# Early loads issued behind the last transposed keys, and one more stage between an expert's gather and its transposes

## The chip, the cores and the metric

The kernel runs on one core of one Trainium2 chip. The metric is the device time of the whole program in microseconds (us), as the median of the runs shown. A core has five engines that each work through their own instruction list in order and wait for one another by semaphores: TensorE (PE in the profile), VectorE (DVE), ScalarE (ACT), GpSimd (POOL) and SyncE (SP), which in this kernel only issues DMAs. POOL issues DMAs as well, beside its arithmetic.

## The reference

A layer norm of x (4 sequences of 2048 tokens, 256 wide) feeds two branches whose outputs are added to x: a gated linear attention with 8 heads, and a mixture of 64 experts, of which each token uses 8.

```python
xn = _layernorm(x)
# attention: q, k (8 heads x 128), v (8 heads x 64), alpha = sigmoid((xn @ Wg + bg) / 16)
state = alpha * state + k[..., None] * v[:, None, :]      # step by step over each sequence
out_t = einsum('bhk,bhkv->bhv', q, state)
attn  = (out * sigmoid(xn @ Wog)) @ Wo
# experts, over all n = 8192 tokens
scores = sigmoid(xn @ gate_w.T)
topk_idx = 8 of 64 experts, out of the best 4 of 8 groups (scores + bias decide)
topk_w   = scores of those 8, normalised, times 2.5
pos      = rank of the token among those of its expert, in the order of the tokens
buf[e, pos] = xn[token]  for pos < CAP                    # CAP = 256 rows an expert
y   = einsum(silu(buf @ w_gate) * (buf @ w_up), w_down)
moe[token] += y[e, pos] * topk_w
return x + attn + moe
```

## The kernel before

**Blocks.** The tokens are cut into 32 blocks of 256 (two chunks of 128). `block(s)` does the attention of block s and, between its parts, the projections of block s+1: `gate` (output gate), `values`, `queries` and `keys`, each for a half of the heads. `unit_a` makes the decays and scores of one half and chunk, `unit_m` multiplies them, `unit_d` makes the outputs and the new state. After each part comes a `step()`, twelve in a full block and seven in the last one.

**Side work.** `step()` first runs what lies in `side`: for the first half of the program that is the routing (`front`, `decays`, `back` for 16 batches of 512 tokens). `front` normalises a batch, transposes it with a DMA (`xT`, line 363), stores it, and multiplies it with the router's weights (`lg` on PE). The batches also leave the counts in `cnt_d`, and the rows to be gathered (tokens and weights, 1280 bytes each) in `xw_d`.

**Experts.** When the side work is done (at block 17 of 0 to 31), 64 experts go through a pipeline that `step()` drives: every 12/5 steps a new expert starts, and every expert already under way moves on by one stage. This interval is called a period below. `fetch` issues three loads of the expert's weights (`w`, on SP) and two gathers of its 256 rows (`xe`, indirect DMAs on POOL). The stages that follow are `expert_in` (eight PE transposes of the rows into `xet`, and the split of weights and rows into high and low parts), `expert_mid` (the two products, `gu`, and the activation), `expert_out` (the third product, `yp`, and the scaled rows `y` on ACT), and `expert_add` (two scatter-adds of `y` into the output, on POOL). `behind_adds` makes every scatter-add, and every write of an attention block (`finish`, `out_dram<-res`, on POOL as well), wait until the last two scatter-adds before it have landed. Ahead of the gathers, `look(e)` finds the row numbers of expert e; for each eighth expert (`NF = 8`) `steps` first loads two tables of counts `c` and subtracts them into `dd`. Once all experts have started, they move on by a stage with every step.

**Buffers.** `w` has three buffers, `xe` four, `y` four, `el` three, `xs` two, `c` one of each kind.

**The loads of a block.** `block(s)` opens with `load_block(s+1)` (`xs`, the transposed tokens; `aj` and `mv`, the decay vectors) and `load_el(s+1, 0)`; `load_el(s+1, 1)` comes after the second half of the keys. `el` is 512 KB, read by `queries` (`qt` on DVE) and by the copies `wall`, which are on POOL for blocks below 16 and on DVE above. `keys` ends with a DMA that transposes the keys of a half (`kt`, line 837), which `unit_d` multiplies.

**Order.** Tile's scheduler fixes each engine's order when the program is built, from the dependences and from when it takes each instruction to be ready; a load whose buffer is free can thus stand on SP well ahead of its place in the text. `tc.issue_after(ins)` adds the rule that what the block traces on the engine of `ins` is issued after `ins`, without a wait for it to finish.

Of the kernel before, what the change touches and what calls it, by code (L numbers as in the profile page):

```python
# [8 lines left out]
F32 = mybir.dt.float32  # L9
# [10 lines left out]
P = 128  # L20
NT = 8192
NTL = NT // 128
# [3 lines left out]
E, CAP, I = 64, 256, 128  # L26
# [10 lines left out]
XW = D + E  # L37
# [15 lines left out]
DGROUPS = ((0, 1), (1, 1), (2, 2), (4, 4), (8, 4), (12, 4))  # L53

STEPS = 12
NF = 8
AHEAD = 2
EXPERTS = 5

# [10 lines left out]
def gla_moe_kernel(ctx: ExitStack, tc: tile.TileContext, x, Wq, Wk, Wv, Wo, Wg, bg, Wog,  # L70
                   gate_wT, gate_bias, w_gate, w_up, w_down, out):
    nc = tc.nc
# [10 lines left out]
    cnt_d = dram.tile([(NTL + 1) * E, P], F16, name="cnt_d")  # L83
# [31 lines left out]

    dd_t = [const.tile([NTL, NF, P + 2], F16, name=f"dd{i}") for i in range(2)]

# [22 lines left out]
    made = {}  # L140
# [404 lines left out]

    moe = {}

    def steps(g):

        both = []  # L550
        for t in range(2):
            c = moe["m1"].tile([NTL, NF, P], F16, name=f"c{t}")
            nc.sync.dma_start(out=c, in_=cnt_d[t * E:(t + NTL) * E, :].rearrange(
                "(t e) i -> t e i", e=E)[:, g * NF:(g + 1) * NF, :])
            both.append(c)
        nc.vector.tensor_tensor(dd_t[g % 2][:, :, 0:P], both[1], both[0], ALU.subtract)

    def find(e):

        m2 = moe["m2"]
        before = m2.tile([NTL, CAP], F16, name="before")
        nc.vector.tensor_scalar(before, srow, cex[:, e:e + 1], None, ALU.is_ge)
        row = ps["mo"].tile([P, 2, P + 1], F32, tag="mo", name="row")
        for f in range(2):
            nc.tensor.matmul(row[:, f, :], lhsT=before[:, f * P:(f + 1) * P],
                             rhs=dd_t[e // NF % 2][:, e % NF, 0:P + 1], start=True, stop=True)
        le_ = m2.tile([P, 2, P], F16, name="le_")
        place = m2.tile([P, 2], F32, name="place")  # L570
        for f in range(2):
            nc.vector.tensor_scalar(le_[:, f], row[:, f, 0:P], slot[:, f:f + 1], None, ALU.is_le, ALU.add,
                                    accum_out=place[:, f:f + 1])
        nc.vector.tensor_tensor(idx[:, e], row[:, :, P], place, ALU.add)

    def look(e):
        if e < E:
            if e % NF == 0:
                steps(e // NF)
            find(e)  # L580

    def fetch(e):
        w4 = moe["w4"]
        w = w4.tile([P, 6, I], F32, name="w", bufs=3)
        nc.sync.dma_start(out=w[:, 0:2], in_=w_gate[e].rearrange("(c p) i -> p c i", p=P))
        nc.sync.dma_start(out=w[:, 2:4], in_=w_up[e].rearrange("(c p) i -> p c i", p=P))
        nc.sync.dma_start(out=w[:, 4:6].rearrange("p c i -> p (c i)"), in_=w_down[e])
        xe = w4.tile([P, 2, XW], F32, name="xe", bufs=4)
        for f in range(2):
            nc.gpsimd.indirect_dma_start(  # L590
                out=xe[:, f, :], out_offset=None, in_=xw_d[:, :],
                in_offset=bass.IndirectOffsetOnAxis(ap=idx[:, e, f:f + 1], axis=0))
        return dict(w=w, xe=xe)

    def expert_in(e, m):

# [33 lines left out]
    def expert_split(e, m):  # L630
        hh = moe["m2"].tile([P, CAP], F32R, name="hh")
        hl = moe["m2"].tile([P, CAP], F32R, name="hl")
        nc.scalar.copy(hh, m["hs"])
        moe["late"].append((nc.vector, hl, m["hs"], hh))
        m["h"] = (hh, hl)
# [31 lines left out]
        tc.declare_no_dep(two[1], two[0], reason="the halves of an expert share no row")  # L667
        adds.extend(two)

    expert_stages = [expert_in, expert_mid, expert_out, expert_add]  # L670

    def expert_late():

# [4 lines left out]
    def expert_step(new):  # L678

        q = moe["at"]  # L680
        mids = []
        for it in list(q):
            e, m, st = it
            if st == len(expert_stages):
                continue
            expert_stages[st](e, m)
            if st == 1:
                mids.append((e, m))
            it[2] += 1
        for e, m in mids:  # L690
            expert_split(e, m)
        moe["at"] = [it for it in q if it[2] < len(expert_stages)]
        if new and moe["next"] < E:
            e = moe["next"]
            moe["at"].append([e, fetch(e), 0])
            moe["next"] += 1
            look(e + AHEAD + 1)
# [29 lines left out]
    def begin_block(s):  # L727
        blk[s] = dict(el=[None, None], wall=[None, None], q=[None, None], k=[None, None], kt=[None, None],
                      v=[None] * NCK, vw=[None] * NCK, oT=[None] * NCK)
        blk[s]["aux"] = nc.gpsimd if s < NB else nc.vector  # L730
        b, c0 = s // 2, (s % 2) * NCK
        if s == 0:
            xs = batch[0]["xT"][:, 0:NCK]
        else:
            xs = xsp.tile([P, NCK, 2, 2, P], F16, name="xs")
            nc.sync.dma_start(out=xs, in_=xT_d[b][:, c0:c0 + NCK])
        blk[s]["x"] = xs[:, :, 0], xs[:, :, 1]

    def load_block(s):
        if s:  # L740
            begin_block(s)
        b, c0 = s // 2, (s % 2) * NCK
        aj = aj_t[s % 2]
        lt = lt_d[b].rearrange("a h c i -> (a h) c i")
        nc.sync.dma_start(out=aj[0:NJ], in_=lt[0:NJ, c0:c0 + NCK, :])
        nc.sync.dma_start(out=aj[NJ + 2 * NPART:KL], in_=lt[NJ:2 * NJ, c0:c0 + NCK, :])
        mv = []
        for ck in range(NCK):
            t = mv_t[(s * NCK + ck) % NM]
            loaded = nc.sync.dma_start(out=t[NJ:NJ + 2 * NPART], in_=lt_d[b][:, :, c0 + ck, :])  # L750
            mv.append(t)
        blk[s].update(loaded=loaded, aj=aj, mv=mv)

    def load_el(s, half):
        b, c0 = s // 2, (s % 2) * NCK
        el = elp.tile([P, NCK, 4, P], F32, name="el")
        gi = max(i for i, g in enumerate(DGROUPS) if g[0] <= b)
        r0 = ((b - DGROUPS[gi][0]) * RT + c0) * H
        src = el_d[gi][r0:r0 + NCK * H, :].rearrange("(c h) i -> c (h i)", h=H)[:, half * 4 * P:(half + 1) * 4 * P]
        nc.sync.dma_start(out=el.rearrange("p c h t -> p c (h t)"), in_=src.partition_broadcast(P))  # L760
        blk[s]["el"][half] = el
# [65 lines left out]
    def keys(s, half, i):  # L827

        B = blk[s]
        if i == 0:  # L830
            B["k"][half] = qk.tile([P, NCK, 2, 4, P], F16, name="k")
        k = B["k"][half]
        pj = project(s, "wk", (half * 4 + 2 * i) * DK, DK)
        split(two_heads(k[:, :, 0], i), two_heads(k[:, :, 1], i), pj, DK ** -0.5 * KFIT)
        if i == 1:
            kt = ktp.tile([P, NCK * 2 * 4, P], F16, name="kt")
            nc.sync.dma_start(out=kt, in_=k.rearrange("p c a h t -> p (c a h t)"), transpose=True)
            B["kt"][half] = kt

    def unit_a(s, half, ck):  # L840
# [106 lines left out]
    def block(s):  # L947


        n = s + 1 < NS  # L950
        if n:
            load_block(s + 1)
            load_el(s + 1, 0)
        unit_a(s, 0, 0)
        if n:
            queries(s, 1, 0)
        else:
            keys(s, 1, 0)
        unit_m(s, 0, 0)
        step()  # L960
        if n:
            keys(s, 1, 0)
        else:
            keys(s, 1, 1)
        step()
        unit_d(s, 0, 0)
        if s:
            output(s - 1, 0)
            output(s - 1, 1)
        step()  # L970
        if s:
            finish(s - 1)

        unit_a(s, 0, 1)
        queries(s, 1, 1 if n else 0)
        unit_m(s, 0, 1)
        step()
        if n:
            keys(s, 1, 1)
        else:  # L980
            queries(s, 1, 1)
        if n:
            load_el(s + 1, 1)
            gate(s + 1, 0)
        step()
        unit_d(s, 0, 1)
        step()

        if not n:
            unit_a(s, 1, 0)  # L990
            unit_m(s, 1, 0)
            unit_a(s, 1, 1)
            unit_d(s, 1, 0)
            split_o(s, 0)
            unit_m(s, 1, 1)
            output(s, 0)
            unit_d(s, 1, 1)
            split_o(s, 1)
            step()
            return  # L1000
        unit_a(s, 1, 0)
        gate(s + 1, 1)
        unit_m(s, 1, 0)
        step()
        values(s + 1, 0)
        queries(s + 1, 0, 0)
        step()
        unit_d(s, 1, 0)
        split_o(s, 0)
        step()  # L1010

        unit_a(s, 1, 1)
        keys(s + 1, 0, 0)
        unit_m(s, 1, 1)
        step()
        queries(s + 1, 0, 1)
        keys(s + 1, 0, 1)
        values(s + 1, 1)
        step()
        unit_d(s, 1, 1)  # L1020
        split_o(s, 1)
        step()
# [140 lines left out]
```

## Time and profile before

| | |
|---|---|
| median of 3 runs | 1265.52 us (1262.99 to 1268.77) |
| the profiled execution's own time | 1273.01 us |
| its span, first to last instruction | 1271.1 us |
| mean granted TensorE clock | 0.984 |
| PE busy, share of the span | 1175.8 us, 93% |
| DVE busy | 958.6 us, 75% |
| ACT busy | 756.1 us, 59% |
| POOL busy | 755.0 us, 59% |
| loads of `w` from SP | 64 x 3, 128 KB each |
| loads of `el` from SP | 64, 512 KB each |
| loads of `c` from SP | 16, 128 KB each |
| gathers and scatter-adds from POOL | 128 and 128 |

The busy time of an engine is the time in which at least one of its instructions ran; a DMA's time is not part of it, only the time that POOL spends issuing an indirect one. The rows of groups give a line of the kernel, the engine, what is written from what, the busy time with the mean of one, and then the idle time just before, with what ended it. Where an instruction waits for several things, the last one by the profile is named. In the timeline a row has its start, its length, and in brackets the idle time ahead of it. The span has two parts: up to about 585 us attention runs beside the routing, from there beside the experts; the last gather is issued at 1212.63 us, and after the last expert only attention is left.

### The profile page before, as it was taken

To read this page: it belongs to the slowest core of one execution; us is meant where nothing else is said; L and a number is where in the kernel's file an instruction comes from. 1 tells how busy PE (TensorE), PEld (TensorE's weight loads), DVE (VectorE), ACT (ScalarE), POOL (GpSimd) and SP (SyncE) were. 2 spreads that over 40 slices of the span, in tenths; PEclk is the share of its full clock that TensorE was granted. 3 is DMA by queue.
4 is the path that set the end of the run, shared out by engine and by line. 5 is a ranking of instruction groups with operands and counts; after the bars stand their busy time and mean duration, and the time that the engine had idled before them with its cause. 6 is when DMAs were issued, how large, how long until landed. Compare 5 with 4: busy or idle time off the path is not lost.

```text
span 1271.1 us, 32324 instructions
## 1 busy us (share of the span) xinstructions
PE 1175.8 (93%) x12420; PEld 959.4 (75%) x12421; DVE 958.6 (75%) x2685; ACT 756.1 (59%) x1454; POOL 755.0 (59%) x958
## 2 busy tenths in 40 slices
PE   3798889999999999999999999999799998997998
PEld 2577677777777777787888888878688887876786
DVE  7967656767668667867898889877588886885766
ACT  4656656755666656645566666665466654664554
POOL 3377657766777667642257557665567565664541
PEclk9999989999999999999999999999899998999899
DMA  7759776767777676747678787988788878799744
GB/s 222 180 117 255 177 169 153 179 166 164 171 178 175 146 151 148 163 93 189 127 169 168 175 178 155 177 174 152 144 171 171 166 158 161 152 172 145 134 63 84
DMA packets 313255, 203.28 MB, mean 160 GB/s; under 512 B 198507, under 2 KB 283627, under 8 KB 312845
## 3 DMA queue, kind: packets, MB, share of 16 engines
q1 hardware_dynamic: 280365, 155.59, 52.0%
q0 software_dynamic: 32736, 45.63, 22.8%
q8 instruction: 97, 1.59, 0.5%
q14 instruction: 57, 0.47, 0.1%
HBM read 112.57 MB, written 54.71 MB: 132 GB/s over the span
## 4 chain that ended last, share of the span: by engine, by line
PE 54%; DMA 15%; DVE 12%; POOL 9%; issue 5%; ACT 4%; SPq 1%; POOLq 0%; DVEq 0%; ACTq 0%
PE pj L254 9%; PE pj L256 9%; PE pj L255 9%; DMA xe<-xw_d,idx 6%; DMA el<-el_d 4%; PE od L887 4%; PE od L891 3%; PE xet L603 2%; DMA xT<-x 2%; PE gu L254 2%; PE gu L255 2%; PE gu L256 2%; PE lp L847 2%; PE sp L254 2%; DVE qt L818 2%
## 5 line engine op out<-in xcount | busy, mean ns | idle before, releaser
L661 POOL DMA_INDIRECT out_dram<-y,idx x128 | 221.7, 1732 | 201.0 <-ACT y L647 49.5
L590 POOL DMA_INDIRECT xe<-xw_d,idx x128 | 141.5, 1105 | 49.3 <-issue 30.8
L254 PE MATMUL pj<-xs,wk_h 128*128 128x256 f16 x496 | 136.6, 275 | 0.0
L254 PE MATMUL pj<-xs,wq_h 128*128 128x256 f16 x496 | 136.5, 275 | 0.0
L256 PE MATMUL pj<-xs,wq_l 128*128 128x256 f16 x496 | 136.4, 275 | 0.0
L255 PE MATMUL pj<-xs,wq_h 128*128 128x256 f16 x496 | 136.4, 275 | 0.0
L256 PE MATMUL pj<-xs,wk_l 128*128 128x256 f16 x496 | 136.3, 275 | 0.0
L255 PE MATMUL pj<-xs,wk_h 128*128 128x256 f16 x496 | 136.2, 274 | 0.0
L870 DVE TENSOR_TENSOR dc<-sp,dc 128x512 f32<-128x512 f32 x128 | 87.6, 684 | 61.0 <-POOL dc L857 51.0
L887 PE MATMUL od<-dc,v 128*64 128x128 f32 x1024 | 110.8, 287 | 9.6 <-DVE dc L870 8.6
L205 ACT ACTIVATE qh<-pj 128x512 f16<-128x512 f32 x128 | 76.4, 597 | 63.0 <-PE pj L256 62.7
L206 DVE SCALAR_TENSOR_TENSOR ql<-pj,qh 128x512 f16<-128x512 f32 x128 | 87.2, 681 | 28.8 <-ACT qh L205 28.3
L891 PE MATMUL od<-qt,state 128*64 128x128 f32 x960 | 101.9, 276 | 0.0
L205 ACT ACTIVATE k<-pj 128x512 f16<-128x512 f32 x128 | 75.9, 593 | 42.3 <-PE pj L256 41.5
L254 PE MATMUL sp<-qh,k 128*128 128x128 f16 x512 | 97.3, 222 | 0.0
L255 PE MATMUL sp<-ql,k 128*128 128x128 f16 x512 | 96.6, 221 | 0.3 <-DVE ql L206 0.3
L206 DVE SCALAR_TENSOR_TENSOR k<-pj,k 128x512 f16<-128x512 f32 x128 | 86.8, 679 | 13.1 <-ACT k L205 12.6
L256 PE MATMUL sp<-qh,k 128*128 128x128 f16 x512 | 96.0, 221 | 0.0
L851 ACT ACTIVATE dc<-lp 128x512 f32<-128x512 f32 x128 | 76.5, 598 | 30.7 <-PE lp L847 30.6
L675 DVE TENSOR_TENSOR wl<-w,wh 128x768 fp32r<-128x768 f32 x64 | 61.2, 956 | 37.9 <-ACT wh L607 36.9
L887 PEld LDWEIGHTS od<-dc,v 128*64 128x64 f32 x1024 | 60.7, 136 | 37.6 <-issue 11.1
L818 DVE SCALAR_TENSOR_TENSOR qt<-pj,el 128x512 f32<-128x512 f32 x128 | 86.7, 678 | 2.6 <-DMA el<-el_d 2.6
(395 smaller groups left out, 4258.8 us busy)
## 6 DMA issues: line engine op xcount, KB each, us to landing
el<-el_d SPq DMA_DIRECT2D x64, 512.0 KB
xw_d<-x SPq DMA_DIRECT2D x16, 512.0 KB
xT_d<-xT SPq DMA_DIRECT2D x16, 512.0 KB
out_dram<-in_L_attn_x_dram SPq DMA_DIRECT2D x16, 512.0 KB
w<-in_L_ffn_w_gate_dram SPq DMA_DIRECT2D x64, 128.0 KB
w<-in_L_ffn_w_up_dram SPq DMA_DIRECT2D x64, 128.0 KB
w<-in_L_ffn_w_down_dram SPq DMA_DIRECT2D x64, 128.0 KB
xs<-xT_d SPq DMA_DIRECT2D x31, 256.0 KB
```

The costliest lines, as they stand in the source:

```text
L205: return (nc.scalar.activation(hi, t, AF.Copy, scale=scale).ins, nc.vector.scalar_tensor_tensor(lo, in0=t, scalar=scale, in1=hi, op0=ALU.m ...
L206: nc.vector.scalar_tensor_tensor(lo, in0=t, scalar=scale, in1=hi, op0=ALU.mult, op1=ALU.subtract).ins)
L254: nc.tensor.matmul(out_, lhsT=a[0], rhs=b[0], start=first, stop=False)
L255: nc.tensor.matmul(out_, lhsT=a[0], rhs=b[1], start=False, stop=False)
L256: return nc.tensor.matmul(out_, lhsT=a[1], rhs=b[0], start=False, stop=last).ins
L590: nc.gpsimd.indirect_dma_start(out=xe[:, f, :], out_offset=None, in_=xw_d[:, :], in_offset=bass.IndirectOffsetOnAxis(ap=idx[:, e, f:f + 1] ...
L661: two = [nc.gpsimd.indirect_dma_start(out=of, out_offset=bass.IndirectOffsetOnAxis(ap=idx[:, e, f:f + 1], axis=0), in_=m["y"][:, f, :], in ...
L818: read = nc.vector.scalar_tensor_tensor(qt, in0=pj, scalar=QFIT, in1=two_heads(el, i), op0=ALU.mult, op1=ALU.mult)
L851: nc.scalar.activation(dc, lp, AF.Relu, scale=-1.0)
L870: anchor.append(nc.vector.tensor_tensor(dc, B["sp"], dc, ALU.mult).ins)
L887: nc.tensor.matmul(op[i * DV:(i + 1) * DV, j, :], lhsT=v[:, h0 + 2 * j + i, :], rhs=dc[:, 2 * j + i, :], start=True, stop=first)
L891: nc.tensor.matmul(op[i * DV:(i + 1) * DV, j, :], lhsT=state[half][:, 2 * j + i, :], rhs=qt[:, ck, 2 * j + i, :], start=False, stop=True)
```

## The change

The tables of counts hold four experts and not eight, so `steps` runs sixteen times with half the bytes each. A new stage `expert_weights` stands ahead of `expert_in`: `fetch` issues the gathers alone, the loads of `w` are issued a period later, and the transposes of an expert's rows come another period after that. `xe` gets a fifth buffer. `keys` keeps its last `kt` instruction in `made["kt"]`, and the loads of `c`, of `w`, of a next block (`xs`, `aj`, `mv`) and of `el` are issued on SP after the `kt` that was traced last before them.

```diff
--- before.py
+++ after.py
@@ -53,7 +53,7 @@
 DGROUPS = ((0, 1), (1, 1), (2, 2), (4, 4), (8, 4), (12, 4))
 
 STEPS = 12
-NF = 8
+NF = 4
 AHEAD = 2
 EXPERTS = 5
 
@@ -545,13 +545,18 @@
 
     moe = {}
 
+    def behind_keys():
+
+        return tc.issue_after(made["kt"]) if "kt" in made else ExitStack()
+
     def steps(g):
 
         both = []
         for t in range(2):
             c = moe["m1"].tile([NTL, NF, P], F16, name=f"c{t}")
-            nc.sync.dma_start(out=c, in_=cnt_d[t * E:(t + NTL) * E, :].rearrange(
-                "(t e) i -> t e i", e=E)[:, g * NF:(g + 1) * NF, :])
+            with behind_keys():
+                nc.sync.dma_start(out=c, in_=cnt_d[t * E:(t + NTL) * E, :].rearrange(
+                    "(t e) i -> t e i", e=E)[:, g * NF:(g + 1) * NF, :])
             both.append(c)
         nc.vector.tensor_tensor(dd_t[g % 2][:, :, 0:P], both[1], both[0], ALU.subtract)
 
@@ -580,17 +585,20 @@
             find(e)
 
     def fetch(e):
-        w4 = moe["w4"]
-        w = w4.tile([P, 6, I], F32, name="w", bufs=3)
-        nc.sync.dma_start(out=w[:, 0:2], in_=w_gate[e].rearrange("(c p) i -> p c i", p=P))
-        nc.sync.dma_start(out=w[:, 2:4], in_=w_up[e].rearrange("(c p) i -> p c i", p=P))
-        nc.sync.dma_start(out=w[:, 4:6].rearrange("p c i -> p (c i)"), in_=w_down[e])
-        xe = w4.tile([P, 2, XW], F32, name="xe", bufs=4)
+        xe = moe["w4"].tile([P, 2, XW], F32, name="xe", bufs=5)
         for f in range(2):
             nc.gpsimd.indirect_dma_start(
                 out=xe[:, f, :], out_offset=None, in_=xw_d[:, :],
                 in_offset=bass.IndirectOffsetOnAxis(ap=idx[:, e, f:f + 1], axis=0))
-        return dict(w=w, xe=xe)
+        return dict(xe=xe)
+
+    def expert_weights(e, m):
+        w = moe["w4"].tile([P, 6, I], F32, name="w", bufs=3)
+        with behind_keys():
+            nc.sync.dma_start(out=w[:, 0:2], in_=w_gate[e].rearrange("(c p) i -> p c i", p=P))
+            nc.sync.dma_start(out=w[:, 2:4], in_=w_up[e].rearrange("(c p) i -> p c i", p=P))
+            nc.sync.dma_start(out=w[:, 4:6].rearrange("p c i -> p (c i)"), in_=w_down[e])
+        m["w"] = w
 
     def expert_in(e, m):
 
@@ -667,7 +675,7 @@
         tc.declare_no_dep(two[1], two[0], reason="the halves of an expert share no row")
         adds.extend(two)
 
-    expert_stages = [expert_in, expert_mid, expert_out, expert_add]
+    expert_stages = [expert_weights, expert_in, expert_mid, expert_out, expert_add]
 
     def expert_late():
 
@@ -684,7 +692,7 @@
             if st == len(expert_stages):
                 continue
             expert_stages[st](e, m)
-            if st == 1:
+            if st == 2:
                 mids.append((e, m))
             it[2] += 1
         for e, m in mids:
@@ -834,7 +842,7 @@
         split(two_heads(k[:, :, 0], i), two_heads(k[:, :, 1], i), pj, DK ** -0.5 * KFIT)
         if i == 1:
             kt = ktp.tile([P, NCK * 2 * 4, P], F16, name="kt")
-            nc.sync.dma_start(out=kt, in_=k.rearrange("p c a h t -> p (c a h t)"), transpose=True)
+            made["kt"] = nc.sync.dma_start(out=kt, in_=k.rearrange("p c a h t -> p (c a h t)"), transpose=True).ins
             B["kt"][half] = kt
 
     def unit_a(s, half, ck):
@@ -949,8 +957,9 @@
 
         n = s + 1 < NS
         if n:
-            load_block(s + 1)
-            load_el(s + 1, 0)
+            with behind_keys():
+                load_block(s + 1)
+                load_el(s + 1, 0)
         unit_a(s, 0, 0)
         if n:
             queries(s, 1, 0)
@@ -980,7 +989,8 @@
         else:
             queries(s, 1, 1)
         if n:
-            load_el(s + 1, 1)
+            with behind_keys():
+                load_el(s + 1, 1)
             gate(s + 1, 0)
         step()
         unit_d(s, 0, 1)
```

## The prediction

> **What bounds the kernel now.** I read the busy table and the chain of the page, then PE's waits, busy time by stretch, and the timelines of POOL and DVE.
>
> ```profile
> PE 54%; DMA 15%; DVE 12%; POOL 9%; issue 5%; ACT 4%; SPq 1%; POOLq 0%; DVEq 0%; ACTq 0%
> PE pj L254 9%; PE pj L256 9%; PE pj L255 9%; DMA xe<-xw_d,idx 6%; DMA el<-el_d 4%; PE od L887 4%; PE od L891 3%; PE xet L603 2%; DMA xT<-x 2%; PE gu L254 2%; PE gu L255 2%; PE gu L256 2%; PE lp L847 2%; PE sp L254 2%; DVE qt L818 2%
> ...
> L661 POOL DMA_INDIRECT out_dram<-y,idx x128 | 221.7, 1732 | 201.0 <-ACT y L647 49.5 <-issue 29.8 <-DMA out_dram<-res 29.7
> L590 POOL DMA_INDIRECT xe<-xw_d,idx x128 | 141.5, 1105 | 49.3 <-issue 30.8 <-DVE dc L855 10.7 <-PE pj L256 2.4
> ```
>
> PE leads the chain, but gathers (`xe`, 6%) and POOL (9%) stand in it too. PE's waits, and busy time by stretch (second column PE, fifth POOL, then granted clock, DMA share):
>
> ```profile
> PE lg L254 <- DMA xT<-x: 28.5, 16, 9.8
> PE xet L603 <- DMA xe<-xw_d,idx: 27.9, 13, 6.1
> ...
> PE od L254 <- DMA kt<-k: 3.7, 2, 3.0
> ```
> ```profile
> 662.00:790.00 128.00, 128.00 (x1335) 107.98 (x1332) 108.96 (x284) 81.43 (x168) 84.19 (x60) 1.00 0.83 171
> 790.00:1000.00 210.00, 199.68 (x2043) 166.51 (x2043) 165.95 (x433) 125.28 (x257) 129.77 (x90) 0.98 0.84 166
> 1000.00:1212.00 212.00, 194.31 (x1953) 161.89 (x1951) 161.44 (x413) 119.88 (x249) 128.97 (x91) 0.95 0.83 151
> ```
>
> From 662 to 790 PE never stops; later it loses time, all of it ahead of `xet`, and clock too. Why is `xe` late? The gather of expert e stands on POOL behind the scatter-add of e-4:
>
> ```profile
> 1099.89 2.69 POOL L661 DMA_INDIRECT out_dram<-y,idx  x1 [5.50 <-ACT qh L205]
> 1102.89 1.82 POOL L661 DMA_INDIRECT out_dram<-y,idx  x1 [0.30 <-issue]
> 1105.02 1.02 POOL L590 DMA_INDIRECT xe<-xw_d,idx  x1 [0.30 <-issue]
> 1106.35 0.98 POOL L590 DMA_INDIRECT xe<-xw_d,idx  x1 [0.30 <-issue]
> 1107.88 1.62 POOL L661 DMA_INDIRECT out_dram<-y,idx  x1 [0.55 <-issue]
> ```
>
> The name in the first bracket misleads: the `y` of that pair was ready at 1096.22 on ACT. By the packet records the pair before landed at 1098.64, and 1.25 later this one goes. This holds pair after pair: from 783 to 1248 nearly every pair and every `out_dram<-res` starts about 1.2 us after the last landing; only 18.9 us in all are waits beyond that. So a second bound lies beside PE: the **chain of adds**. `out_dram<-res`, one a block, is issued at 657.19, 702.69, 746.77, 790.47 (44.4 us a block, PE's pace), but over the next eight blocks, to 1185.51, at 49.4 us a block: as landings lengthen (mean of eight pairs 5.9 us at first, 7.9 for the last but one eight), the chain falls 5.0 x 8 = 40 us behind PE. PE pays it in waits for `xe`: 27.9 us, and half of 27.3 us at half clock, 13.7, together 41.6.
>
> At the end both meet. SP's load of `mo`, which waits for the last adds, is issued at 1248.03; DVE waits for it:
>
> ```profile
> 1250.82 0.43 DVE L943 TENSOR_TENSOR mo<-mo,res 128x256 f32<-128x256 f32 x1 [1.05 <-DMA mo<-out_dram]
> ...
> 1258.48 0.41 DVE L900 SCALAR_TENSOR_TENSOR oT<-og,od 128x256 f32<-128x256 f32 x1
> ```
>
> **The change, part by part.** Instruction orders are those of the two built programs.
>
> *The extra stage.* POOL's order goes from "adds 36, gather 40" to "adds 36, gather 41": each gather stands behind adds that are one expert older. A fifth `xe` buffer holds what is in flight for a period longer; no instruction is added. A period is 44.4/5 = 8.9 us of PE. So PE may run one period further ahead of the adds before it waits. That is gained once: 41.6 - 8.9 = 32.7 us of loss stay, and **PE's path** ends 8.9 us sooner.
>
> *The chain of adds* gets a later start. The first matmul of `yp` for expert 16 stands at place 7077 of PE's order before and 7233 after; 156 matmuls at 0.104 us (1335 records in 128 us, 0.918 of a listed matmul each) are 16 us. In the old run the adds of expert 16, at 783.10, started with their `y`, so they follow it 16 us later. From there the chain runs without pause, as PE is ahead. It can win back only waits for a late `y`: at most the 18.9 us above. I take four fifths, 15, since some were waits for `res`. Last landing: 1248.0 + 16 - 15 = 1249.0.
>
> *The tail.* The two adds of `mo` move back on DVE's list, to just behind the `oT` that ran at 1258.48 to 1258.89. From there to the end of the span were 12.2 us. The chain's end is then 1249.0 + 2.8 (load to first use) + 0.9 (two adds) + 12.2 = 1264.9. PE's path, 1271.1 - 8.9 = 1262.2, is shorter. After `yp` of the last expert three decay products (`lp`) are still to come on PE in both orders, so the fifth stage's drain does not reach the end.
>
> *Clock.* The granted clock falls to half for 3.4 to 10.2 us after waits. The Trainium skill, "TensorE: Matmul & The Clock Gate", Part 1, puts the fall after an idle window of about 3.4 us. Here shorter ones did it:
>
> ```profile
> 1202.80:1205.40 2.60, 0.02 (x1) 0.00 (x0) 2.50 (x6) 1.58 (x4) 1.99 (x3) 1.00 1.13 147
> 1205.50:1208.90 3.40, 3.40 (x19) 2.52 (x19) 1.29 (x3) 1.25 (x3) 2.35 (x2) 0.50 0.45 114
> ```
>
> By the rule, waits cut below 3.4 us would give all 13.7 us back and PE's path would end near 1271.1 - 8.9 - 13.7 = 1248.5; by the rows they go on costing clock. I keep the rows; the chain decides either way.
>
> *Loads behind the keys.* `xs`, `aj`, `mv` and the first `el` of a block were issued half a block early, as soon as a buffer was free; now they follow the last `kt`. For block 12 that `kt` leaves SP at 421.6, against 397.2 for `xs` and 398.4 for `el` before. First use on DVE is at 441.7, and a load takes some 5 us to its use (`xs` issued 841.59, 3.4 in the chain; `el` up to 9.3). Over all `el`, 28 to 68 DVE instructions now lie between the keys' split and the first use (53 to 162 before): at 0.42 us each (118 in 50 us) at least 12 us. PE's own first use of `xs` is `gate`, whose `og` on ACT follows that `kt` by 11 us at the least (122.8 to 133.8); less 5 for the load and 3.5 for its products, 2.5 are left. When `kt` waits for its keys, all these loads now wait behind it on SP, and for them `gate` on PE, `qt` and `dd` on DVE, `wh` on ACT. I see no stall in these margins: cost 0; the cover is the work on keys and queries in between. What it wins is small, as PE waits for `kt` only 3.7 us. The second `el`, 512 KB, now goes out right ahead of `xT`, whose matmuls `lg` wait 1.2 to 2 us a batch. From issue to `lg` is 4.4 us with nothing ahead. Bounds over 14 batches: 1 us each later, +14; or, since `lg` stands 0.5 us of PE work later and `wall` (POOL waited 44.0 us for `el`) no longer stands before the high-low split of x, -7. I take 0.
>
> *Smaller tables.* Sixteen loads more at 0.57 us are 9 us of SP in 630. The skill's "DMA: Bandwidth & Descriptors", Rules for kernel authors, speaks against halving to 64 KB: below that one pays mostly overhead.[...] The row is that DVE waited for `c` once, 3.0 us, with 9 instructions between the keys' split and the subtraction. Now there are 13 to 31 (up to 173 before), so 0 by that row, at most 16 x 3.0 = 48 on an engine that idles 15% there. I take 0. DVE's subtractions for `dd` keep their sum, 5.4 us.
>
> *The weights* are loaded and cast a period later together: their distance is unchanged. From the fifth expert on 17 ACT instructions or more, at 0.8 us each (62 in 50 us), lie between the split of the keys ahead and the cast: 0.
>
> **Sum.** The profiled span goes from 1271.1 to 1264.9: -6.2 us. This execution took 1273.01, 7.5 above the median of 1265.52; the difference is taken off the median: **1259.3**.
>
> **The rivals.** *PE's path alone:* if landings shorten, as the loads of a block no longer come in the middle of others, the chain stops binding and the clock returns: 1248.5 by the rule above, 1243 as a median. Against it: landings grew with traffic that stays the same. *Slower, the chain:* the 16 us of late start are paid and nothing is won back, since the old waits for `y` only turn into longer landings. Place: POOL, expert 16 to 63. The end is 1248.0 + 16 + 2.8 + 0.9 + 12.2 = 1279.9, +8.8, or 1274 as a median. It decides once less than 8.8 of the 18.9 us come back; 47 pairs that each land 0.14 us later than I reckon would do it. For it: DMA share 0.83 all through. *Slower, the first half:* `el` and `kt` in one burst hold up `xT` and, on POOL, `wall`: +14 by the bound, and the saving of 6 then leaves +8, 1273. *Nothing happens:* excluded by the orders, which do change.
>
> **How the numbers follow.** The sum as told 0.5 (own range 1252 to 1267), PE's path alone 0.17, slower by the chain 0.2, slower by the first half 0.13. A measurement of this kernel tells about 0.5%, 6.3 us, from no change. Of the first case about half falls beyond, of the slower ones 0.27 of 0.33: faster 0.42, same 0.31, slower 0.27. Range 1242 to 1279: the cases' ends, with a tenth left out on each side.
>
> **What would show it.** Right: waits of `xet` for `xe` fall to near 18 us and start later than 807; adds still go 1.2 us after a landing, first pair at about 648, last landing near 1249; DVE waits for `mo`. Wrong: a last landing beyond 1256, more than 35 us of `lg` waiting for `xT`, DVE waiting for `c` or `el` by 10 us or more.

## The result, and the profile after

The changed kernel took 1273.01 us (median of 4 runs, 1271.74 to 1274.04) where the kernel before, on the same chip, took 1264.52 (4 runs): a ratio of 1.0061, 95% interval 1.0034 to 1.0089. It is slower by some 8 us. The forecast was 1259.3. (Ratios, here and below, leave out executions more than 1.5% above the fastest of their kernel, while medians take all of them, so the two need not agree.)

The profiled execution of the changed kernel has a span of 1272.3 us and took 1274.04, 1.0 above its median. First the chain of the page (shares by engine, then by line):

```profile
PE 55%; DMA 14%; DVE 9%; POOL 9%; ACT 5%; issue 5%; SPq 2%; POOLq 0%; DVEq 0%; ACTq 0%
PE pj L254 9%; PE pj L256 9%; PE pj L255 9%; DMA xT<-x 4%; PE od L895 3%; DMA c<-cnt_d 3%; PE od L899 3%; PE gu L254 2%; PE gu L256 2%; PE gu L255 2%; PE xet L611 2%; PE sp L254 2%; PE lp L855 2%; DMA out_dram<-y,idx 1%; PE sp L255 1%
```

The gathers (`xe`, 6% before) have left the list, and the loads of the tables `c` (3%) are new in it. PE's waits of the changed kernel say the same of the gathers (who waits, for whom: us in total, times, longest):

```profile
PE lg L254 <- DMA xT<-x: 27.3, 12, 9.9
PE od L895 <- DVE dc L878: 17.2, 8, 13.6
PE xet L611 <- DMA xe<-xw_d,idx: 12.9, 7, 3.8
...
PE od L254 <- DMA kt<-k: 0.5, 1, 0.5
```

`xet` waits 12.9 us for `xe` instead of 27.9, `od` 0.5 instead of 3.7 for `kt`. So on PE the change does what it was meant to do, as far as one pair of profiles can tell. But a new line has come: `od` waits for `dc` from DVE, 13.6 us of it in one piece. The stretches of the prediction, and two at the end (second column PE, fifth POOL, then clock, DMA share):

```profile
662.00:790.00 128.00, 127.75 (x1324) 107.42 (x1324) 109.12 (x284) 80.40 (x167) 79.65 (x56) 1.00 0.79 173
790.00:1000.00 210.00, 200.94 (x2038) 166.28 (x2035) 167.00 (x440) 125.71 (x257) 128.26 (x90) 0.98 0.79 162
1000.00:1212.00 212.00, 205.03 (x2096) 171.89 (x2095) 169.33 (x435) 125.89 (x265) 137.31 (x96) 0.98 0.83 164
1244.40:1258.10 13.70, 0.11 (x4) 0.06 (x2) 3.01 (x7) 0.66 (x2) 4.44 (x3) 0.61 0.55 103
1258.10:1272.30 14.20, 9.58 (x68) 8.59 (x68) 3.90 (x8) 1.98 (x4) 0.00 (x0) 0.62 0.06 19
```

From 1000 to 1212 PE works 205.03 us instead of 194.31, at a clock of 0.98 instead of 0.95. Near the end it stands still for 13.7 us, and does the rest at 0.62 of its clock. DVE's timeline shows what it waits for (start, duration, operation, and in brackets the idle time before it and who ended it):

```profile
1243.26 0.41 DVE L908 SCALAR_TENSOR_TENSOR oT<-og,od 128x256 f32<-128x256 f32 x1
1255.09 0.76 DVE L951 TENSOR_TENSOR mo<-mo,res 128x256 f32<-128x256 f32 x2 [11.42 <-DMA mo<-out_dram]
1255.77 0.68 DVE L863 TENSOR_TENSOR dc<-dc,u_le 128x512 f32<-128x512 f32 x1
```

The `oT` that ran at 1258.48 in the old execution runs at 1243.26: PE is 15 us ahead of that execution. Behind it stand the two adds of `mo`, and those wait for the load of `mo`, which waits for the last scatter-add. Behind them stand the last two pairs of decay products, which PE needs. The chain that ended last, in order of time, goes through all of it (start, us, what):

```profile
1246.49 1.56 POOL out_dram L669
1248.05 0.30 issue
1248.35 3.81 DMA out_dram<-y,idx
1252.42 2.65 DMA mo<-out_dram
1255.09 0.76 DVE mo L951 x2
1255.85 0.60 DVE dc L863
...
1258.05 0.69 PE od L895 x4
```

The chain of adds, not PE, sets this end, and by way of one DVE queue PE has to do its last products after it.

### The profile page after: what moved, and what is told of

Read it like the earlier page. It is cut to its first block, busy times and chain, and to the rows that moved or that the text cites. A ratio compares the mean times of both kernels' runs of the same rounds, so it can differ in the third digit from the quotient of the medians.

```text
span 1272.3 us, 32200 instructions
## 1 busy us (share of the span) xinstructions
PE 1180.2 (93%) x12421; PEld 962.1 (76%) x12421; DVE 956.0 (75%) x2693; ACT 753.1 (59%) x1454; POOL 756.9 (59%) x958
## 3 DMA queue, kind: packets, MB, share of 16 engines
q1 hardware_dynamic: 281645, 155.59, 49.5%
## 4 chain that ended last, share of the span: by engine, by line
PE 55%; DMA 14%; DVE 9%; POOL 9%; ACT 5%; issue 5%; SPq 2%; POOLq 0%; DVEq 0%; ACTq 0%
PE pj L254 9%; PE pj L256 9%; PE pj L255 9%; DMA xT<-x 4%; PE od L895 3%; DMA c<-cnt_d 3%; PE od L899 3%; PE gu L254 2%; PE gu L256 2%; PE gu L255 2%; PE xet L611 2%; PE sp L254 2%; PE lp L855 2%; DMA out_dram<-y,idx 1%; PE sp L255 1%
## 5 line engine op out<-in xcount | busy, mean ns | idle before, releaser
L669 POOL DMA_INDIRECT out_dram<-y,idx x128 | 224.9, 1757 | 193.2 <-issue 25.7
L254 PE MATMUL sp<-qh,k 128*128 128x128 f16 x512 | 98.9, 224 | 1.1 <-ACT k L205 1.1
L205 ACT ACTIVATE k<-pj 128x512 f16<-128x512 f32 x128 | 76.2, 596 | 36.1 <-PE pj L256 34.7
L256 PE MATMUL sp<-qh,k 128*128 128x128 f16 x512 | 97.4, 223 | 0.0
L860 ACT ACTIVATE dc<-dc 128x512 f32<-128x512 f32 x128 | 81.1, 633 | 2.3
```

The lines of the kernel that those rows point to most:

```text
L205: return (nc.scalar.activation(hi, t, AF.Copy, scale=scale).ins, nc.vector.scalar_tensor_tensor(lo, in0=t, scalar=scale, in1=hi, op0=ALU.m ...
L254: nc.tensor.matmul(out_, lhsT=a[0], rhs=b[0], start=first, stop=False)
L256: return nc.tensor.matmul(out_, lhsT=a[1], rhs=b[0], start=False, stop=last).ins
L669: two = [nc.gpsimd.indirect_dma_start(out=of, out_offset=bass.IndirectOffsetOnAxis(ap=idx[:, e, f:f + 1], axis=0), in_=m["y"][:, f, :], in ...
L860: nc.scalar.activation(dc, dc, AF.Exp, scale=-1.0)
```

## The experiments

Two theories. **A, the tail:** the chain of adds starts a period later, regains little of it and so ends late; an instruction that waits for it stands in a queue that PE still needs. **B, the body:** the loads behind the keys, or the smaller tables, cost time earlier. A third, C, is chance.

Single executions of one program turned out to spread widely: 59 runs of the kernel before on one chip went from 1242 to 1279 us, with a standard deviation of 6.5. So the ratios below are between kernels run in turn on one chip, and a profile is read for its structure, not for its time. The experiments ran in four sets (e1 to e4, e5 to e8, e9 to e12, e13 to e15), each on a chip of its own; the medians of the kernel before were 1260.66, 1267.16, 1264.80 and 1263.59.

| | part of the change | tail | median | less before | ratio, 95% interval |
|---|---|---|---|---|---|
| e3 | stage, tables | as built | 1273.41 | +12.8 | 1.0037, 1.0008 to 1.0067 |
| e4 | gates | as built | 1268.01 | +7.3 | 1.0065, 1.0038 to 1.0092 |
| e5 | all | as built | 1271.32 | +4.2 | 1.0049, 1.0020 to 1.0077 |
| e14 | all | as built | 1269.08 | +5.5 | 1.0071, 1.0039 to 1.0103 |
| e8 | none | `mo` last on DVE | 1267.02 | -0.1 | 1.0023, 0.9996 to 1.0050 |
| e6 | stage, tables | `mo` last on DVE | 1265.94 | -1.2 | 0.9977, 0.9937 to 1.0018 |
| e7 | gates | `mo` last on DVE | 1282.87 | +15.7 | 1.0160, 1.0110 to 1.0211 |
| e2 | all | clear | 1257.68 | -3.0 | 0.9998, 0.9968 to 1.0029 |
| e12 | all | clear | 1261.24 | -3.6 | 0.9975, 0.9950 to 1.0001 |
| e15 | all | clear | 1263.49 | -0.1 | 1.0007, 0.9983 to 1.0030 |
| e11 | none | clear | 1264.11 | -0.7 | 0.9994, 0.9968 to 1.0020 |
| e10 | stage, tables | clear | 1263.09 | -1.7 | 0.9927, 0.9895 to 0.9959 |
| e9 | gates | clear | 1266.31 | +1.5 | 0.9995, 0.9966 to 1.0025 |
| e13 | all, third `res` | clear | 1265.95 | +2.4 | 1.0019, 0.9985 to 1.0053 |

"Clear" means that nothing PE needs stands behind a wait for the last adds, neither on DVE nor on SP. "Gates" are the loads behind the keys.

**e1: the kernel before again**, to see what the 7.5 us were by which its first profile lay above the median.

> The kernel before, unchanged, for a second profiled execution: the first took 7.5 us more than the median of its runs, the one of the changed kernel only 1.0 more. Theory A (the loss lies in the tail: the chain of adds ends late and mo, waiting for it, holds DVE and PE): the extra 7.5 us of the old profile were waits for xe and the clock lost behind them, that is the chain of adds; an ordinary execution has a span near 1262, its last add lands near 1240 and its PE waits for xe less than 20 us. Theory B (the loss lies in the loads behind the keys): the last add lands near 1247 again, and the 7.5 us are found before 600 us, in which case the changed kernel's first half has lost about 8 us against an ordinary execution of the old one.

Span 1250.5, last landing 1226.7. PE's waits in this execution:

```profile
PE lg L254 <- DMA xT<-x: 26.6, 15, 10.0
PE xet L603 <- DMA xe<-xw_d,idx: 14.1, 15, 1.9
```

In the two other profiles of the old order `xet` waits 20.1 us (e8) and 19.0 us (e11). So a third to a half of the 27.9 us that the prediction set out from was that one execution's. The expectation of A holds in kind, if by more than it said: this execution was itself 8 us below the median of its set. Part of the 20 us between the two executions also lay before 200 us, where the first was 6.6 behind (the 17th `oT` at 195.2 against 188.6).

**e2, e12, e15: the changed kernel with `mo`'s adds last on DVE.** PE, ACT, POOL and SP keep their order; on DVE the two adds move from ahead of the last decay products to behind the last `ol` (and one of these products moves by one place).

```
-        if s:
+        if s and n:
             finish(s - 1)
...
             split_o(s, 1)
             step()
+            finish(s - 1)
...
-                nc.vector.tensor_tensor(mo[:, t], mo[:, t], res[:, t], ALU.add)
+                with tc.issue_after(made["ol"]):
+                    nc.vector.tensor_tensor(mo[:, t], mo[:, t], res[:, t], ALU.add)
```

> The changed kernel; only the two adds of mo of block 30 move on DVE, from ahead of the last two decay products to behind the last subtraction for ol. Theory A: PE's gap of 13.6 us ahead of od goes, and with it the half clock at the end (4.2 us); the three remaining decay products follow at about 1244, PE is done near 1256, the last add lands near 1252 as before, and the end is set by the load of mo: span about 1259.5, time about 1260.5, 12 us below the changed kernel and 4 below the kernel before. Theory B (the loads behind the keys, or the tables, cost the time earlier): PE only swaps the wait, as the load of mo comes at the same time and everything up to 1243 is as it was; no more than the 4 us of clock come back, 1268 or more.

> The changed kernel with mo's adds last on DVE (its loads of mo stand behind the last kt on SP as built), again, beside the other three. It was 3.1 us below the kernel before in the mean. Theory A: 2 to 5 us below the kernel before and as fast as the stage with a clear tail or faster, the end set by the last landing plus some 12 us. If it is slower than the stage with a clear tail by 4 us or more, the gates do cost in the body of the run.

> The changed kernel with mo's adds last, on the same chip as the changed kernel itself. Theory A: 3 to 5 us below the kernel before, 8 to 11 below the changed kernel; span ends 11 us after the last landing.

DVE and PE in e12, first DVE's timeline, then PE's waits:

```profile
1238.05 0.69 DVE L926 TENSOR_TENSOR ol<-oT,oh 128x512 fp32r<-128x512 f32 x1 [0.69 <-ACT oh L925]
1244.23 0.76 DVE L952 TENSOR_TENSOR mo<-mo,res 128x256 f32<-128x256 f32 x2 [5.48 <-DMA mo<-out_dram]
```
```profile
PE od L895 <- DVE dc L878: 5.7, 7, 1.5
PE pj L254 <- DVE qt L826: 4.9, 4, 2.0
PE xet L611 <- DMA xe<-xw_d,idx: 2.9, 6, 1.0
```

`mo` still waits, 5.48 us, but nothing that PE needs waits for it. PE's long gap is gone (longest wait of `od` 1.5). The span ends 11.1, 11.2 and 11.0 us after the last landing in the three, where it was 20.5 in the first profile of the changed kernel.

**e5, e14: the changed kernel itself, in more runs.**

> The changed kernel, unchanged, in more runs and beside the kernel before, since single executions of one program turned out to differ by some 6 us either way. Theory A (tail: the chain of adds ends late, mo holds DVE and PE): 8 to 12 us over the kernel before, with DVE waiting for mo by 8 us or more and PE's longest gap late in the run right behind it. Theory C (chance of the few runs): within 3 us of the kernel before.

> The changed kernel on the same chip as the two with mo last, for a direct comparison. Theory A: 8 to 11 us slower than with mo's adds last, 4 to 8 slower than the kernel before; span ends 19 to 21 us after the last landing. If it is within 4 us of mo last, the gain seen on different chips was the chips'.

Chance (C) falls: with the first result three sets give 1.0049 to 1.0071. In e5 the loss is less than the 8 to 12 us that A put there, 4.2 by the medians and some 6 by the ratio. On the chip where both ran, `mo` last is 5.6 us faster (1263.49 against 1269.08, medians), less than the 8 to 11 that A put there, and not the 3 to 5 below the kernel before. Against the kernel before, `mo` last is 0 to 3.6 us faster by the medians, with three ratios whose intervals all hold 1: the loss is taken away, a gain isn't shown. DVE waited 6.9 and 6.1 us for `mo` in the two profiles, and `od` on PE up to 9.1 and 8.3 right behind.

**e3: the stage, the fifth `xe` buffer and the tables without the gates** (`behind_keys` returns an empty `ExitStack()`).

> The extra stage, the fifth xe buffer and the smaller tables, but no load is kept behind the keys. mo of block 30 stands on DVE ahead of two decay products and an oT, as in the kernel before. Theory A: first pair of adds near 650, chain without a pause to about 1252, PE some 10 us ahead of the kernel before; DVE waits for mo by 12 us or more, PE with it, and the end is 1270 to 1276. Theory B (the gates are what costs): faster than the kernel before, about 1259.

By the medians it lies 12.8 us above the kernel before, as A has it; by the ratio, which rests on 10 of its 20 runs, only some 5. DVE waits for `mo` 9.8 us, less than the 12 expected, and PE up to 5.5 behind it. `mo` stands still further ahead on DVE here:

```profile
1238.00 0.43 DVE L951 TENSOR_TENSOR mo<-mo,res 128x256 f32<-128x256 f32 x1 [9.82 <-DMA mo<-out_dram]
1238.34 0.41 DVE L908 SCALAR_TENSOR_TENSOR oT<-og,od 128x256 f32<-128x256 f32 x1
```

**e6, e10: the same with `mo`'s adds last, then with the tail clear** (e10 also puts both loads of `mo` behind the last `kt` on SP).

```
-            behind_adds(nc.sync.dma_start(out=mo, in_=dst).ins)
+            with tc.issue_after(made["kt"]):
+                behind_adds(nc.sync.dma_start(out=mo, in_=dst).ins)
```

> The extra stage, the fifth xe buffer and the smaller tables without the gates (as in the run of the stage alone, 1274.0 in the mean against 1261.3 for the kernel before), and the adds of mo of block 30 behind the last ol on DVE. Theory A: the stage's loss of 12.7 us was the tail, so it falls to the time of the changed kernel with mo last, 1258, give or take 3. Theory B (the loss is spread over the run): no more than 5 us come back, 1269 or more.

> The extra stage and the smaller tables without gates, with the tail cleared on both queues. With mo's adds last on DVE alone it was 0.5 us below the kernel before, and PE still waited 2.2 us for the one kt behind mo's load. Theory A: 2 to 5 us below the kernel before, the end set by the last landing (first pair near 650, last landing 6 to 12 us later than in the kernel before) plus some 12 us. Theory B: no change from 0.5 below.

By the medians the 12.8 us come back: 1.2 below the kernel before in e6, 1.7 in e10. By the ratios 1.0037 becomes 0.9977 and 0.9927. In the profile of e10 DVE no longer waits for `mo`, and the span ends 15.0 us after the last landing, not some 12. Taken at its word, the ratio of e10, 0.9927 (0.9895 to 0.9959), would make it faster than both kernels, and some 6 us faster than e12 of the same set; a lead of 4 us or more had been named ahead, for e12, as the sign that the gates cost in the body. But the ratio rests on 10 of 22 runs, and which ones they are hangs on the fastest (1243.45), 4.7 us ahead of the next. By the medians of all runs e10 is 1.9 us slower than e12. Neither is shown.

**e4: the gates alone** (on `xs`, `aj`, `mv`, `el` and `c`, with tables of 8 experts and four stages; the weights stay with the gather).

> The kernel before with xs, aj, mv, both el and the tables c (of 8 experts) kept behind the last transposed keys; four stages, weights loaded with the gather as before. Theory A: first pair of adds near 635 and last landing within 3 us of the kernel before, no gap in the tail, time within 4 us of the kernel before. Theory B: 6 to 9 us slower than the kernel before, with the loss in waits for xT, el or c before 600 us.

7.3 us slower: what B had said. But B's loss before 600 us isn't there: the 65th `oT` on DVE comes at 583.0, among the 581.9 to 587.8 of the old order. SP's timeline in e4, and PE's behind it, show a place that neither theory had named:

```profile
1230.34 0.38 SPq L946 DMA_DIRECT2D mo<-out_dram  x1
1230.82 10.09 SPq L842 DMA_TRANSPOSE kt<-k  x2
```
```profile
1241.39 0.24 PE L254 MATMUL od<-vwh,kt 128*128 128x64 f16 x1 [3.48 <-DMA kt<-k]
```

In this build the load of `mo`, which waits for the last adds, stands on SP ahead of the last two `kt`. It is the hold-up of A, on another queue.

**e7, e9: the gates with `mo`'s adds last, then with the tail clear on both queues.**

> The gates on xs, aj, mv, el and c alone, four stages (1268.7 in the mean against 1261.3), and the adds of mo behind the last ol. This build also issues the load of mo on SP behind the last two transposed keys instead of ahead of them; in the profile of the gates alone the last kt stood behind that load and PE waited 3.5 us for it. Theory A: most of the 7.4 us was this tail, so within 3 us of the kernel before. Theory B (the gates cost in the body of the run, in waits for xT, el, c or kt): 5 us or more over the kernel before.

> The gates alone, with the tail cleared on both queues: mo's adds last on DVE, and both loads of mo on SP behind the last transposed keys (in the two runs of the gates before this one the first load of mo, which waits for the last adds, stood ahead of the last two kt; what was written ahead of the second of them, that its load stands behind the kt, was a misreading of the order). Theory A (a wait for the last adds put into a queue that PE still needs hands the chain's lateness to PE): PE no longer waits for kt by 3 to 7 us late in the run, the span ends within 24 us of the last landing instead of 34, and the time is within 3 us of the kernel before. Theory B (gates cost in the body): 5 us or more over the kernel before.

e7 is a miss for A: 15.7 us slower, in six runs. Moving the adds alone leaves the last two `kt` behind the load of `mo` on SP (I had misread the order when I wrote the expectation), and PE waited 7.2 us for one. With the load behind them (e9) PE waits 0.6 us in all for `kt` and the ratio is 0.9995, as A has it. The span still ended 28.5 us after the last landing (34.7 in e4, 34.2 in e7), against the 24 expected; what fills the rest isn't known. Why e7 is 8 us worse than e4 I can't say: up to the tail the two have the same order, but e7's first pair of adds went out 15 us later (654.4 against 639.2), and it ran on another chip.

**e8, e11: the kernel before with `mo`'s adds last, and with a clear tail.**

> The kernel before with the adds of mo behind the last ol (and its load behind the last kt on SP). In the kernel before the last add lands 17 us ahead of PE's end, and DVE waits only 1.1 us for mo. Theory A: 0 to 3 us below the kernel before. If it gains 6 us or more, the tail cost the kernel before as well, and the gain of the changed kernel with mo last over it is not the change's.

> The kernel before with the tail cleared on both queues: the reference for the other three. Its adds land 17 us ahead of PE's end, so both theories expect no more than 2 us either way.

No effect (1.0023 and 0.9994): the old kernel had nothing to clear, as its adds land 23.7 to 24.0 us ahead of its end.

**e13: a third `res` buffer besides.**

```
-            B["res"] = w2.tile([P, NCK, D], F32, name="res")
+            B["res"] = w2.tile([P, NCK, D], F32, name="res", bufs=3)
```

> The changed kernel with mo's adds last on DVE and, besides, a third res buffer. With two, the last res copies on ACT (block 31) waited 9.3 us for the write of block 29's res, which POOL sends only behind the last adds; the span ended 11.2 us after the last landing. Theory A (what is left at the end is the chain of adds and what is queued behind it): res is copied when PE is done, the span ends 7 to 8 us after the last landing (load of mo 2.8, four adds 1.5, store 2 to 3), and the time falls 3 to 4 us below that of mo's adds last alone. Rival (the end is PE's): no change.

No gain. The copies of `res` on ACT no longer wait, but the span still ends 11.0 us after the last landing: POOL's last write of `res` stands behind the last adds, lands 5.0 after its issue, and the span ends 5.1 after that landing, in e12, e13 and e15 alike. What fills these 5.1 us isn't known.

## Why the prediction was wrong

Each profile's span is read here as the sum of three parts: the time to the first pair of adds, the length of the chain from there to its last landing, and what follows. By the packet records, in us:

```
                          first pair   last landing   span     chain   after it
before (first profile)      635.5        1247.4       1271.1   611.9     23.7
before (e1)                 631.7        1226.7       1250.5   595.0     23.8
before, mo last (e8)        635.0        1238.6       1262.6   603.6     24.0
before, clear (e11)         634.4        1237.7       1261.4   603.3     23.7
changed (first profile)     647.8        1251.8       1272.3   604.0     20.5
changed (e5)                651.4        1247.0       1266.5   595.6     19.5
changed (e14)               652.8        1249.4       1269.9   596.6     20.5
changed, mo last (e2)       646.4        1239.6       1250.7   593.2     11.1
changed, mo last (e12)      649.0        1240.8       1252.0   591.8     11.2
changed, mo last (e15)      655.2        1257.2       1268.2   602.0     11.0
```

In the profiles that are not in the table the last column is 22.5 (e3), 19.8 (e6), 15.0 (e10), 34.7 (e4), 34.2 (e7), 28.5 (e9) and 11.0 (e13). Within the kernel before, within the changed one and within the changed one with `mo` last it hardly moves, while the landings move by up to 20 us. That alone would also fit a chain that follows PE. But from the adds of expert 16 to the last ones, some 450 us, the waits of a link (a pair of adds, or a write of `res`) beyond 1.25 us after the landing ahead of it come to only 10.6 to 17.7 us in the four profiles of the old order, and to 3.4 to 4.9 in the three of the changed kernel. So in both kernels it is the chain of adds that sets the time. In the old one PE is tied to it by the gathers, and ends a fixed 24 us after it. The extra stage loosens that tie, PE runs ahead, and the chain comes to the end nearly alone.

*The late start: right at the first pair, too small at expert 16.* 16 us were forecast. The changed kernel's three profiles start at 650.7 in the mean, the four of the old order at 634.2: 16.5. The `y` of expert 16 comes 17.6 us later in these means. Its adds, for which the 16 us were reckoned, come 25.3 us later, because they no longer start with their `y`; in the first profile, after 783.10 in the old one:

```profile
796.22 0.84 ACT L655 ACTIVATE y<-yp,xe 128x256 f32<-128x256 f32 x2
808.52 1.65 POOL L669 DMA_INDIRECT out_dram<-y,idx  x1 [4.74 <-ACT y L655]
```

(The name in the bracket misleads again: the `y` was ready at 797.1. A write of `res`, issued at 802.42, now stands ahead of this pair.) The chain is full from its first pair on, and not from expert 16: in the first sixteen experts its waits are 1.9 to 4.6 us, against 9.4 to 13.9 in the old order.

*The step that failed first: "It can win back only waits for a late `y`", of which "four fifths, 15" were taken.* The waits did go. Of POOL's idle time ahead of the adds, ACT's `y` ended most before, 49.5 us, and is no longer among the first three after:

```profile
L669 POOL DMA_INDIRECT out_dram<-y,idx x128 | 224.9, 1757 | 193.2 <-issue 25.7 <-ACT xeh L618 25.6 <-DMA out_dram<-y,idx 24.9
```

By the packet records, over the whole chain, the waits beyond 1.25 us after a landing fall from 26.5 us (mean of the four profiles of the old order) to 8.4 (mean of the three of the changed kernel). But the sum kept every landing at its old length, and the landings grew: from issue to last packet, all links together, 503.6 us instead of 491.6. The chain is 598.7 us long instead of 603.5, or instead of 600.6 without the first profile: 2 to 5 us won back, not 15. Waits gave way to longer landings, as the rival "slower, the chain" has it. Why the landings grew was not traced; the runs with the extra stage alone have 494.7 to 507.3 us of them (e3, e6, e10), those with the gates alone 487.5 to 495.5 (e4, e7, e9).

*The last landing: right by luck.* 1249.0 was forecast; 1251.8, 1247.0 and 1249.4 were measured, 1249.4 in the mean. The forecast started from the one old execution whose chain was the longest (611.9, against 595.0 to 603.6 in the other three). Against the mean of all four, 1237.6, the last landing moved by 11.8 us.

*"The difference is taken off the median"* then turned this into an error of the time. The step takes the changed kernel's end, reckoned on the profiled execution, to lie as far above its median as that execution did: 7.5 us. That is fair only where the gain holds for an ordinary execution. But that execution had 31.6 us of waits in its chain where the other three had 20.0 to 28.3: part of its bad luck was counted twice, once as waits to win back, once as a distance to the median. Without the deduction the forecast would have been 1264.9 + 1.9 = 1266.8.

*The second step that failed: the 12.2 us "from there to the end of the span".* They were measured where DVE came to that place late and PE ran at full clock. I had PE gain 8.9 us and `mo` land at 1249, but did not reckon what DVE's wait there does to PE. DVE waited 11.4, 6.9 and 6.1 us for `mo`, PE stood 13.6, 9.1 and 8.3 us, and from the end of the first `mo` adds to the end of the span it was 16.5 us in the first profile. The end came 20.2 us after the last landing in the mean of three, where the sum had 15.9. The prediction gives `mo` its place on DVE's list and names no one behind it; that sentence is the one that was missing.

*Both together.* The forecast was -6.2 us: the last landing 1.6 later than in the old profile (1247.4 by the packets), the stretch after it 7.8 shorter. By the means the landing came 11.8 later and the stretch got 3.6 shorter: +8.2, as the medians have it (+8.5). So the chain is off by 10.2 us and the tail by 4.2.

*PE's path: right in kind.* -8.9 forecast. The `oT` of 1258.48 stands at 1248.8 in the mean of the four profiles of the old order, and at 1242.1 in the mean of the seven of the changed one (e13 with them): -6.7. `xet` waits 12.9, 7.5 and 13.2 us for `xe`; about 18 was forecast, from the same execution.

*Clock: right to keep the rows.* In the changed kernel's first profile a gap of 2.3 us was again followed by half clock (idle stretch, then the next; clock is the last but two):

```profile
94.90:97.20 2.30, 0.04 (x2) 0.00 (x0) 0.24 (x1) 1.70 (x4) 1.90 (x3) 0.98 1.20 232
97.20:100.50 3.30, 3.25 (x46) 3.26 (x47) 1.36 (x4) 1.23 (x2) 0.35 (x2) 0.50 1.18 303
```

The idle window of about 3.4 us that the Trainium skill states ("TensorE: Matmul & The Clock Gate", Part 1) is thus no safe distance here. The longest piece at half clock was in a place I had not costed at all: 20.5 us, by the clock records, from 1247.4 on. It begins within the 13.6 us gap of the tail, where it costs nothing; only its last 9.9 us lie on PE's work behind the gap (0.62 in the stretch above), and at half clock can cost half of that, some 5 us.

*Loads behind the keys: cost 0, and none seen in the body.* `lg` waits 27.3 us for `xT` (28.5 before), DVE 2.8 for `el`, and the 65th `oT` comes at 583.6 to 585.4 in the changed kernel's profiles, 581.9 to 587.8 in the old order's. With a clear tail the gates alone are at 0.9995. As built alone they cost 7.3 us, which the clear tail takes away, on another chip. That e10 by its ratio is ahead of e12 leaves a cost beside the stage open.

*Smaller tables: the sign set for "wrong" came; its price isn't shown.* DVE waited for `c` 37.8 us in 15 places of 16, near the upper bound of 48:

```profile
DVE dd L561 <- DMA c<-cnt_d: 37.8, 15, 5.1
```

PE's `row` waited 0.3 us for it, which speaks for DVE's idle time as cover enough; yet the loads of `c` are 3% of the chain that ended last, and no run had the tables alone. The row I went by, one wait of 3.0 us in the old execution, said little about loads that go out only behind the keys.

*The rivals.* "Slower, the chain" came: 1274 was forecast for it, and its point of decision, less than 8.8 us won back, is where the runs lie. It deserved more than 0.2. That its number lies so near is in part luck, as it took nothing to be won back and lacked the 4.2 us of the tail; the wait of DVE for `mo` was among the signs to look for, never a cost. "The first half" and "PE's path alone" did not come.

## What to carry to other kernels

Where one engine is tied to a chain of transfers, loosening the tie moves the chain's lateness to the end of the program; then look through every in-order queue for an instruction that waits for the chain's last landing, and ask what stands behind it. Here two adds on DVE were worth 5.6 us on one chip (e14 to e15), and with the load of `mo` on SP besides the gates went from 1.0065 to 0.9995 (e4 to e9, on two chips); putting them last cost nothing (e8, e11). A link that no longer waits for its data can take longer to land, so a pause in such a chain is not a gain until the landings are summed as well. And before a profile's pauses are counted, profile the same kernel a second time: a stall of an unlucky execution must not be taken both as a gain and as a distance to the median.

## What the runs showed of the hardware

Executions of one and the same program spread more than expected: standard deviations of 5 to 11 us in sets of 14 runs and more, on a span of 1260, in which the mean granted clock goes along (correlation -0.7 between time and clock over the 59 runs of the kernel before in the first set). One run of the kernel before in the last set, which took 1636.7 us at a granted clock of 0.66, is not in these figures. Waits of 2.0 to 2.6 us on PE were followed by 3.4 us at half clock (2.0 in e11, 2.1 in e8, 2.3 in the rows above, 2.6 in the prediction's). Landings of the scatter-adds vary from 5.2 to over 10 us a pair, on a chain that hands every such difference on to its end.
